# Two graph layers on one core: layer 0's later blocks projected in pairs by seven half products

## The chip, the cores and the metric

The kernel runs on one core of one Trainium2 chip. The metric is the device time of one execution in microseconds (us). A core has a matrix engine (TensorE, PE in the profile), a vector engine (VectorE, DVE), an activation engine (ScalarE, ACT), GpSimd (POOL) and SyncE (SP). In this kernel GpSimd issues the gathers and scatters by index, and SyncE issues the plain transfers. Each engine works through its own queue in order.

## The reference

`x` is 2708 x 1024, `adj` is a 2708 x 2708 matrix of zeros and ones in which most entries are zero; all numbers are float32. Cut to what matters:

```
q, k, v = x @ Wq.T + bq, x @ Wk.T + bk, x @ Wv.T + bv
z    = scale * (q @ k.T) * adj              # zeros count as -10000
x1   = layernorm(x + relu(softmax(z) @ v))  # layer 0
out  = layernorm(x1 + adj @ (x1 @ w1) + b1) # layer 1
```

A row without neighbours gets the mean of all rows of v in layer 0.

## The kernel before, in words

The kernel first turns `adj` into lists of neighbours, in the order of the rows' degrees, and then works on 22 row blocks of 128 rows (the last holds 20). `SLOTS` gives the number of neighbours that a block's rows have at most: 15, 11, 8, 6, 5, 4, 3, 2 for blocks 0 to 7, 13 for block 8, then 5, 4, 4, 3, 3, 3, 2, 2, 2, 1, 1, 1 and 0 for blocks 9 to 21. Blocks 0 and 8 are the widest; some rows with very many neighbours (the "hub" rows) have their shares spread over extra rows.

Layer 0 is rearranged so that there are two products per block. With M = Wq^T Wk (scaled, tile `m_sb`), `y_block` computes y = x M for a block and writes it to DRAM (`y_d`; `yo` is its tile). With y a block's scores need no k: `attend` (or `attend_one` for blocks with one slot, `attend_shares` for the hub and block 0) gathers the block's y rows (`yg`, `gather_y`) and its neighbours' x rows (`g`, `gather`), takes each score as a row-wise product on VectorE (`score`), does the softmax on VectorE and ScalarE, and sums the neighbours' x rows with those weights into `r` (ScalarE makes the first term, VectorE adds the others). Because the weights of a row add up to one, softmax @ v = r @ Wv.T + bv. So each block needs one product more: `flip` turns r by eight transposes into `rT`, `project` makes 16 matmuls (two banks of 128x512, eight each) with `wv_sb`, and `finish0` adds bv to the two banks, does relu and the residual in one instruction over 128x1024, normalises (`norm`) and scatters the rows to `x1_d`. Block 21 takes the mean (`project_mean`).

The order of layer 0 is written out in `steps`: ("y", b) is a block of y, ("v", b) a projection. The y rows 8 to 21 alternate with the projections of blocks 6, 5, 4, 3, 2 and 1; behind the last y (block 21) come the projections of 0, 7, 20, 19, 18, 21, 17, 16, 15, 14, 8, 13, 9, 12, 10 and 11. A small planner hands out the gather-and-softmax pieces (`jobs`, and `late_jobs`, which need every row of y and so wait until y ends) beside the steps: each step adds `STEP` = 14.7 to a credit, and each piece takes its estimated VectorE time from it (`SLOT`, `SMALL`, `END`). `RB` = 3 buffers hold the r tiles. Instructions under `tc.high_priority(URGENT)` are put early on their engine's queue: the additions that read a bank are among them.

Neighbours are gathered into 9 buffers (`G1`); once y has ended, a second pool of 6 (`g2`) is added, until layer 1. Behind y, w1's eight row strips are loaded into the slot of M, one per step (line 1005), and one subtraction over 128x2048 (t1, line 1011) prepares layer 1 within layer 0.

Layer 1 (`work1`) projects neighbour sums of x1. It takes blocks in pairs (`units`), where a pair is a 2 x 2 arrangement of halves: with A = (a11 a12; a21 a22), one row of it per block and each half 512 deep, and w1 in quarters (w11 t1; w21 w22), seven half products (`half_products`, 4 matmuls of 128x512 each) stand for eight. For this, four sums and differences of the turned blocks (`S`, lines 1109 to 1112), three more differences of w1's quarters (t2, t3, t4, lines 1178 to 1180) and additions out of the banks on VectorE (lines 1135 and 1140) are needed. All matmuls of layer 1 are on line 1117.

Lines that the prediction uses: 318 matmuls of y, 322 their additions, 348 gathers, 696 transposes, 719 matmuls of `project`, 771 scores, 828 accumulation of r, 864 and 866 bias and relu with residual, 754 to 767 `norm` (767 is its last ScalarE step), 840 and 848 first and later terms of sums with equal weights, 1086 copies of the bias into layer 1's residual tiles, 1079 neighbour sums of layer 1.

Of the kernel before, what the change touches and what calls it, by code (L numbers as in the profile page):

```python
# [31 lines left out]
SLOTS = [15, 11, 8, 6, 5, 4, 3, 2] + [13, 5, 4, 4, 3, 3, 3, 2, 2, 2, 1, 1, 1, 0]  # L32
MIXED = [7]
# [46 lines left out]
def sparse_part(ctx, tc, x, xT, adj, wqT, wkT, wvT, bq, bk, bv, w1, b1, out):  # L80
# [30 lines left out]
    with es:  # L111
# [24 lines left out]
        wq_i = wm_pool.tile([P, DC, D], F32, name="wq_i", tag="m")  # L136
        wk_i = wk_pool.tile([P, DC, D], F32, name="wk_i")
        for c in range(DC):
            nc.sync.dma_start(out=wq_i[:, c, :], in_=wqT[c * P:(c + 1) * P, :])
# [63 lines left out]
        loaded, sorted_, products = [], [], []  # L203
# [31 lines left out]
        wq_o = wv_pool.tile([P, DC, D], F32, name="wq_o", tag="v")  # L235
        wk_o = wb.tile([P, DC, D], F32, name="wk_o")

        def flip_w(dst, src):

            n = 0  # L240
            for c in range(DC):
                for g in range(DC // 4):
                    tr = p_tr.tile([P, 4, P], F32, name="tr")
                    for k in range(4):
                        o = g * 4 + k
                        nc.tensor.transpose(tr[:, k, :], src[:, c, o * P:(o + 1) * P], ident)  # L246
                    to = dst[:, g * 4:g * 4 + 4, c * P:(c + 1) * P]
                    if n % 2:
                        nc.vector.tensor_copy(to, tr)
                    else:  # L250
                        nc.scalar.copy(to, tr)
                    n += 1

        flip_w(wq_o, wq_i)
        flip_w(wk_o, wk_i)
        load_adj()
        load_adj()
        for c in range(DC):
            nc.vector.scalar_tensor_tensor(junk[:, :D], wq_i[:, c, :], scale, bk_bc, op0=ALU.mult,
                                           op1=ALU.mult, accum_out=u_col[:, c:c + 1])  # L260
# [27 lines left out]
        def y_block(b):  # L288
# [9 lines left out]
            if b == NB - 1:  # L298
# [3 lines left out]
                with tc.high_priority(URGENT):  # L302
                    for c in range(DC):
                        for g in range(G):
                            nc.tensor.matmul(po[g * HUB:(g + 1) * HUB, :YW // G], xt[:, c, :HUB],
                                             m_sb[:, c, g * YW // G:(g + 1) * YW // G], start=(c == 0), stop=(c == DC - 1))
# [8 lines left out]
            for h, (k0, k1) in enumerate(y_cuts):  # L315
                po = p_o.tile([P, HALF], F32, name="po")
                for c in range(DC):
                    put = nc.tensor.matmul(po[:, :k1 - k0], xt[:, c, :], m_sb[:, c, k0:k1], start=(c == 0), stop=(c == DC - 1))  # L318
                    if c == 0:
                        firsts.append(put)  # L320
# [186 lines left out]

        def sort_begin(f):
# [84 lines left out]
        m_sb = wm_pool.tile([P, DC, YW], F32, name="m_sb", tag="m")  # L593
        nc.vector.memset(m_sb[:, :, D:], 0.0)
        nc.vector.tensor_copy(m_sb[:, :, D], u_col)
        done = 0
        for i in range(DC):
            for h in range(NH):
                hs = slice(h * HALF, (h + 1) * HALF)
                po = p_o.tile([P, HALF], F32, name="po")  # L600
                for o in range(DC):
                    nc.tensor.matmul(po, wq_o[:, o, i * P:(i + 1) * P], wk_o[:, o, hs],  # L602
                                     start=(o == 0), stop=(o == DC - 1))
                nc.scalar.copy(m_sb[:, i, hs], po)
# [17 lines left out]
        for b in range(FAMILY):  # L622
# [6 lines left out]
            if b == FAMILY - DC // 2 - 3:  # L629
                wv_sb = wv_pool.tile([P, DC, D], F32, name="wv_sb", tag="v")  # L630
            elif FAMILY - DC // 2 - 2 <= b < FAMILY - 2:
                for c in range(2 * (b - FAMILY + DC // 2 + 2), 2 * (b - FAMILY + DC // 2 + 2) + 2):
                    put = nc.sync.dma_start(out=wv_sb[:, c, :], in_=wvT[c * P:(c + 1) * P, :])
                    follow(put, products[-2])
# [14 lines left out]
        gps = [es.enter_context(tc.tile_pool(name="g0", bufs=G1, reuse_waits="tile"))]  # L649
        turns = [0]  # L650
# [5 lines left out]
        def g_tile():  # L656

            turns[0] += 1
            pool = gps[turns[0] % len(gps)]
            return pool.tile([P, D], F32, name="g", tag="g")  # L660

        def g_clear(pool, n):

            for _ in range(n):
                nc.gpsimd.memset(pool.tile([P, D], F32, name="g", tag="g"), 0.0)

        with tc.high_priority(URGENT):
            g_clear(gps[0], G1)
# [45 lines left out]
        def project(rT, w):  # L714
            po = []
            for h in range(NH):
                acc = p_o.tile([P, HALF], F32, name="po")
                for c in range(DC):
                    put = nc.tensor.matmul(acc, rT[:, c, :], w[:, c, h * HALF:(h + 1) * HALF],  # L719
# [5 lines left out]
        def project_mean(rT, w):  # L725

            acc = p_o.tile([P, HALF], F32, name="po")
            with tc.high_priority(URGENT):
                for c in range(DC):
                    for g in range(G):  # L730
                        nc.tensor.matmul(acc[g * HUB:(g + 1) * HUB, :D // G], rT[:, c, :],
                                         w[:, c, g * D // G:(g + 1) * D // G], start=(c == 0), stop=(c == DC - 1))
# [13 lines left out]
        def norm(t, sm, n, sm2=None):  # L746
# [20 lines left out]
            nc.scalar.activation(t[:n], t[:n], AF.Identity, bias=nmr[:n], scale=rstd[:n])  # L767
# [17 lines left out]
        def attend(b, got):  # L785
# [4 lines left out]
            for i, (j0, j1) in enumerate(cut):  # L790
# [33 lines left out]
                else:  # L824
                    r = wp.tile([P, D], F32, name="r", bufs=RB)
# [45 lines left out]
        def attend_shares(b, got):  # L871
# [9 lines left out]
            for i, (j0, j1) in enumerate(pieces(J)):  # L881
# [25 lines left out]
                if i < len(pieces(J)) - 1:  # L907
# [24 lines left out]

        nc.sync.dma_start(out=bias_bc, in_=bv.to_broadcast([P, D]))
        STEP, Y_END, END, SLOT, SMALL = 14.7, 2.8, 3.3, 2.6, 1.5
        got, xb_bc = {}, []
        w1_left = list(range(DC))
# [3 lines left out]
        late_jobs = [7] + single[::-1] + [17, 16, single[2], 15, single[1], 14, single[0], 8, 8, 8, 13, 9, 12, 10, 11]  # L940
# [3 lines left out]
                 ("y", 15), ("v", 2), ("y", 16), ("y", 17), ("v", 1), ("y", 18), ("y", 19), ("y", 20), ("y", 21)]  # L944
        steps += [("v", b) for b in [0, 7] + single[::-1] + last + [17, 16, 15, 14, 8, 13, 9, 12, 10, 11]]
        assert sorted(b for k, b in steps if k == "v") == list(range(NB))
# [18 lines left out]
        credit = 0.0  # L965
        turned = {}
        pending = None
        left_y = NB - FAMILY
        for i, (kind, b) in enumerate(steps):
            if pending is not None:  # L970
                finish0(*pending)
                pending = None
                credit -= END
            credit += STEP
# [7 lines left out]
            ahead = [c for k, c in steps[i:i + 2] if k == "v" and c not in turned]  # L982
            for c in [c for k, c in steps[i:i + 3] if k == "v" and c not in turned and not (left_y and c in late)]:
                while c not in got and c != 0:
                    credit -= run_job()
            while jobs and credit > 0 and len([c for c in got if c not in turned and c not in last and c != "hub"]) < RB - 1:
# [3 lines left out]
            for c in ahead:  # L990
                turned[c] = turn0(c)
            if kind == "y":
# [3 lines left out]
                if left_y == 0:  # L996
                    xa.release()
                    xb_pool = tc.alloc_tile_pool(name="xb", bufs=1, side="right", reuse_waits="tile")
                    xb_bc.append(xb_pool.tile([P, D], F32, name="xb_bc"))
                    bcast_rows(xb_bc[0], xbT)  # L1000
                    gps.append(tc.alloc_tile_pool(name="g2", bufs=6, side="right", reuse_waits="tile"))
                    w1_sb = wm_pool.tile([P, DC, D], F32, name="w1_sb", tag="m")
            if not left_y and i >= 24 and len(w1_left) > 0:
                c = w1_left.pop(0)
                put = nc.sync.dma_start(out=w1_sb[:, c, :], in_=w1[c * P:(c + 1) * P, :])
                follow(put, products[-1])
            if i == len(steps) - 2:

                w11, t1 = w1_sb[:, :DC // 2, :HALF], w1_sb[:, :DC // 2, HALF:]
                w21, w22 = w1_sb[:, DC // 2:, :HALF], w1_sb[:, DC // 2:, HALF:]  # L1010
                nc.vector.tensor_sub(t1, t1, w11)
            if kind == "v":
                xr = gather_x(x, b)
                pending = b, (project_mean if b in last else project)(turned[b], wv_sb), xr
        finish0(*pending)
        assert not jobs and not w1_left
# [35 lines left out]
        gps.pop().release()  # L1052
        xb_pool.release()
        wv_pool.release()
        cp = tc.alloc_tile_pool(name="c", bufs=1, side="right", reuse_waits="tile")
        cq = tc.alloc_tile_pool(name="cq", bufs=1, side="right", reuse_waits="tile")
        t2, t3, t4 = [cq.tile([P, DC // 2, HALF], F32, name=f"t{k}") for k in (2, 3, 4)]
# [4 lines left out]
        assert sorted(last + [b for unit in units for b in unit]) == list(range(NB))  # L1062
        firsts = []
# [18 lines left out]
        def gather_x1(b, k=0):  # L1082
# [3 lines left out]
            nc.scalar.copy(xr[:n], bias1[:n])  # L1086
# [12 lines left out]
        def turn1(unit, rs):  # L1099

            A = []
            for b, r in zip(unit, rs):
                rT = (cp if A else wp).tile([P, DC, P], F32, name="rT", bufs=2)
                A.append(flip_shares([(part, to_h), (r, to_0)], rT) if b == 0 else flip(r, rT))
            if len(unit) == 1:
                return A, None
            (a11, a12), (a21, a22) = [(a[:, :DC // 2], a[:, DC // 2:]) for a in A]
            S = [cp.tile([P, DC // 2, P], F32, name=f"s{i}") for i in range(4)]
            nc.vector.tensor_add(S[0], a21, a22)
            nc.vector.tensor_sub(S[1], S[0], a11)  # L1110
            nc.vector.tensor_sub(S[2], a11, a21)
            nc.vector.tensor_sub(S[3], a12, S[1])
            return A, S

        def half_products(acc, a, w, start=True, stop=True):
            for k in range(DC // 2):
                nc.tensor.matmul(acc, a[:, k], w[:, k], start=start and k == 0, stop=stop and k == DC // 2 - 1,  # L1117
                                 skip_group_check=True)

        def halves_of(t):  # L1120
            return t[:, :HALF], t[:, HALF:]

        def work1(unit, A, S, xrs):


            ts = [wp.tile([P, D], F32, name="t", tag="t" if k % 2 == 0 else "yg") for k, _ in enumerate(unit)]
            sums = [[stat.tile([P, 1], F32, name=f"sm{h}", bufs=6) for h in range(NH)] for _ in unit]
            a11, a12 = A[0][:, :DC // 2], A[0][:, DC // 2:]

            def bank():  # L1130
                return p_o.tile([P, HALF], F32, name="po")

            def add(to, acc, what):
                with tc.high_priority(URGENT):
                    nc.vector.tensor_add(to, acc, what)  # L1135

            def whole(k, h, acc, what):

# [4 lines left out]
            x0 = halves_of(xrs[0])  # L1143
# [372 lines left out]
```

## Time and profile before

| | us |
|---|---|
| median of 3 runs | 1109.32 |
| lowest and highest run | 1108.97, 1109.59 |
| the profiled execution | 1109.92 |
| span of the profiled execution | 1108.0 |
| TensorE busy | 1033.3 (93%) |
| VectorE busy | 785.7 (71%) |
| GpSimd busy | 473.0 (43%) |
| ScalarE busy | 427.1 (39%) |

The granted clock of TensorE was 0.981 of full speed over the span. Stages, by the span's own clock: lists, M and weights until about 195 us; y of blocks 0 to 7 until about 270; y of blocks 8 to 21 with projections until 555.9; the projections behind y until 786.5; a gap on TensorE until 800.3 with the last normalisation, its scatter and layer 1's first gathers; layer 1's products until about 1090; the last normalisation until 1108.0.

A profile row gives the engine, the line, the operation, output and inputs by the program's names with the shape, the number of instructions or records, and in brackets the idle time ahead of it with what released it. Float32 matmuls leave two records each, so 16 matmuls are "x32".

### The profile page before, as it was taken

To read this page: it belongs to the slowest core of one execution; us is meant where nothing else is said; L and a number is where in the kernel's file an instruction comes from. 1 tells how busy PE (TensorE), PEld (TensorE's weight loads), DVE (VectorE), ACT (ScalarE), POOL (GpSimd) and SP (SyncE) were. 2 spreads that over 40 slices of the span, in tenths; PEclk is the share of its full clock that TensorE was granted. 3 is DMA by queue.
4 is the path that set the end of the run, shared out by engine and by line. 5 is a ranking of instruction groups with operands and counts; after the bars stand their busy time and mean duration, and the time that the engine had idled before them with its cause. 6 is when DMAs were issued, how large, how long until landed. Compare 5 with 4: busy or idle time off the path is not lost.

```text
span 1108.0 us, 10733 instructions
## 1 busy us (share of the span) xinstructions
PE 1033.3 (93%) x3233; PEld 549.3 (50%) x3233; DVE 785.7 (71%) x1712; ACT 427.1 (39%) x896; POOL 473.0 (43%) x397
## 2 busy tenths in 40 slices
PE   7999999999788899999999999999588999999993
PEld 6444466656454455465654444444244444445441
DVE  8799999960677879982166699952268877996531
ACT  4688687312121223232343243332422353323322
POOL 1000320077453456541056377320286778787400
PEclk9999999999999999999999999999798999999997
DMA  9555478426685656644158469521298769989611
GB/s 363 197 203 201 157 241 273 154 77 179 245 275 168 219 187 223 216 142 156 32 186 282 141 211 327 176 97 55 83 282 268 224 188 321 282 271 309 177 46 41
DMA packets 83107, 218.22 MB, mean 197 GB/s; under 512 B 15290, under 2 KB 37274, under 8 KB 80332
## 3 DMA queue, kind: packets, MB, share of 16 engines
q0 software_dynamic: 48768, 148.05, 41.6%
q1 hardware_dynamic: 34272, 69.40, 18.8%
q8 instruction: 27, 0.44, 0.2%
q14 instruction: 40, 0.33, 0.1%
HBM read 208.60 MB, written 33.68 MB: 219 GB/s over the span
## 4 chain that ended last, share of the span: by engine, by line
PE 34%; DVE 25%; issue 18%; DMA 11%; POOL 7%; ACT 2%; POOLq 0%; SPq 0%; DVEq 0%
PE po L719 17%; PE po L318 6%; PE po L1117 6%; DVE a L221 6%; DVE few L224 6%; DMA g<-x_d,tabs 4%; DMA g<-in_x_dram,tabs 3%; POOL g L348 2%; DVE junkv L771 2%; DVE r L1079 2%; PE tr L696 1%; POOL tab_d L558 1%; POOL xr L342 1%; DVE r L828 1%; PE tr L246 1%
## 5 line engine op out<-in xcount | busy, mean ns | idle before, releaser
L318 PE MATMUL po<-m_sb,xt 128*128 128x343 f32 (+1 forms) x1008 | 298.3, 456 | 13.1 <-DVE yo L322 8.3
L719 PE MATMUL po<-wv_sb,rT 128*128 128x512 f32 x672 | 292.3, 593 | 7.0 <-DVE yo L322 3.3
L318 PEld LDWEIGHTS po<-m_sb,xt 128*128 128x128 f32 x1008 | 191.2, 191 | 114.3 <-DVE yo L322 10.9
L719 PEld LDWEIGHTS po<-wv_sb,rT 128*128 128x128 f32 x672 | 126.3, 190 | 161.0 <-issue 154.8
L771 DVE SCALAR_TENSOR_TENSOR junkv<-yg,g 128x1024 uint8<-128x1024 f32 x109 | 132.9, 1219 | 46.4 <-DMA yg<-y_d,tabs 20.0
L348 POOL DMA_INDIRECT g<-in_x_dram,tabs x86 | 106.3, 1236 | 91.1 <-DVE yo L309 28.5
L1079 DVE SCALAR_TENSOR_TENSOR r<-g,valid,r 128x1024 f32<-128x1024 f32 x77 | 98.6, 1281 | 20.2 <-DMA g<-x_d,tabs 19.8
L602 PE MATMUL po<-wk_o,wq_o 128*128 128x512 f32 x256 | 110.5, 592 | 0.0
L754 ACT ACTIVATE junks<-t,lnm 128x1024 uint8<-128x1024 f32 (+1 forms) x43 | 49.4, 1149 | 117.3 <-DVE lnm L750 63.5
L331 ACT ACTIVATE junka<-xt 128x128 f32<-128x128 f32 x176 | 53.9, 306 | 101.4 <-PE po L318 50.9
L1117 PE MATMUL po<-w_sb,rT 128*128 128x512 f32 x192 | 87.2, 598 | 0.0
L348 POOL DMA_INDIRECT g<-x_d,tabs x67 | 76.1, 1136 | 22.7 <-issue 14.0
L828 DVE SCALAR_TENSOR_TENSOR r<-g,pr,r 128x1024 f32<-128x1024 f32 x64 | 81.8, 1279 | 1.6 <-ACT r L826 1.2
L767 ACT ACTIVATE t<-t,nmr,rstd 128x1024 f32<-128x1024 f32 (+1 forms) x43 | 52.9, 1239 | 72.9 <-DVE nmr L766 68.2
L558 POOL DMA_INDIRECT tab_d<-rec,pos_i x22 | 25.1, 1140 | 129.7 <-DVE pos_i L547 123.3
L224 DVE MAX8 few<-a 128x8 f32<-128x75 f32 (+3 forms) x132 | 78.9, 616 | 0.0
L1117 PE MATMUL po<-t,s 128*128 128x512 f32 x160 | 74.5, 610 | 4.0 <-DVE xr L1135 4.0
L602 PEld LDWEIGHTS po<-wk_o,wq_o 128*128 128x128 f32 x256 | 48.4, 190 | 59.3 <-issue 59.0
L1117 PE MATMUL po<-w_sb,s 128*128 128x512 f32 x160 | 72.1, 592 | 0.0
L221 DVE SCALAR_TENSOR_TENSOR a<-a,iota 128x2708 f32<-128x2708 f32 (+1 forms) x22 | 65.2, 2962 | 5.4 <-ACT junk L220 5.4
L864 DVE TENSOR_TENSOR t<-po,bias_bc 128x512 f32<-128x512 f32 (+1 forms) x44 | 30.1, 686 | 50.8 <-PE po L719 50.4
L219 ACT ACTIVATE junk<-a 128x2708 uint8<-128x2708 f32 (+1 forms) x22 | 54.1, 2458 | 28.9 <-DMA a<-in_adj_dram 24.3
(320 smaller groups left out, 1243.1 us busy)
## 6 DMA issues: line engine op xcount, KB each, us to landing
a<-in_adj_dram SPq DMA_DIRECT2D x21, 1354.0 KB, 6.0
y_d<-yo SPq DMA_DIRECT2D x21, 514.0 KB, 6.4
xt<-in_xT_dram SPq DMA_DIRECT2D x21, 512.0 KB, 4.6
wq_i<-in_wqT_dram SPq DMA_DIRECT2D x8, 512.0 KB, 4.5
wk_i<-in_wkT_dram SPq DMA_DIRECT2D x8, 512.0 KB, 11.1
wv_sb<-in_wvT_dram SPq DMA_DIRECT2D x8, 512.0 KB, 6.6
w_sb<-in_w_dram SPq DMA_DIRECT2D x8, 512.0 KB, 3.3
g<-in_x_dram,tabs POOLq DMA_INDIRECT x86, 5.6
```

Source lines behind the costliest of these rows:

```text
L219: nc.scalar.activation(junk[:n], a[:n], AF.Sign, accum_out=cnt[:n, b:b + 1])
L221: nc.vector.scalar_tensor_tensor(a[:n], a[:n], 1.0, iota[:n], op0=ALU.is_equal, op1=ALU.mult)
L224: nc.vector.max(few[:n, i * 8:(i + 1) * 8], a[:n, cuts[i]:cuts[i + 1]])
L318: put = nc.tensor.matmul(po[:, :k1 - k0], xt[:, c, :], m_sb[:, c, k0:k1], start=(c == 0), stop=(c == DC - 1))
L331: put = nc.scalar.activation(junka, xts[b][:, c, :], AF.Copy, accum_out=xs[:, c, b:b + 1])
L348: nc.gpsimd.indirect_dma_start(out=dst[:n], out_offset=None, in_=src, in_offset=bass.IndirectOffsetOnAxis(ap=at, axis=0), bounds_check=N - ...
L602: nc.tensor.matmul(po, wq_o[:, o, i * P:(i + 1) * P], wk_o[:, o, hs], start=(o == 0), stop=(o == DC - 1))
L719: put = nc.tensor.matmul(acc, rT[:, c, :], w[:, c, h * HALF:(h + 1) * HALF], start=(c == 0), stop=(c == DC - 1))
L771: nc.vector.scalar_tensor_tensor(junkv[:n], yg[:n, :D], scale, xg[:n], op0=ALU.mult, op1=ALU.mult, accum_out=s)
L828: nc.vector.scalar_tensor_tensor(r[:n], xg[j][:n], pr[:n, j:j + 1], r[:n], op0=ALU.mult, op1=ALU.add)
L1079: nc.vector.scalar_tensor_tensor(r[:n], xg[:n], ok[:n, j:j + 1], r[:n], op0=ALU.mult, op1=ALU.add)
L1117: nc.tensor.matmul(acc, a[:, k], w[:, k], start=start and k == 0, stop=stop and k == DC // 2 - 1, skip_group_check=True)
```

## The change

Behind the last y the fourteen blocks 7 to 20 go in seven pairs: (7, 20), (19, 18), (17, 8), (16, 11), (15, 10), (9, 14), (13, 12). A pair is computed as in layer 1, by seven half products with the quarters of Wv (11, 12 less 11, 21, 22) and three more differences of them, so four subtractions over 128x2048 are made once, at the first pair. Each pair makes four sums of its turned halves (in one buffer, `s_all`). Its relu, residual and row sum run by halves (`finish_pair`). `pair_products` and `turn_pair` serve both layers; the last pair of either layer runs its products in another order, with a bank of its own for the last one (`first_alone`).

Block 1's projection moves from between y 17 and y 18 to behind y, ahead of block 0's. The planner's credit starts at -`STEP`, a pair adds 2 x `STEP` - `P_END`, the order of `late_jobs` is a new one, and up to three waiting r tiles are allowed behind y (two before). The second neighbour pool (`g2`) is gone: 9 buffers hold the gathers throughout. Block 8's r, and the pair's second rT and t, lie in the pool `xb` that opens when y ends.

Wq, M and Wv are held in four quarter tiles each; Wv arrives in 16 transfers instead of 8. w1 is not loaded into M's slot during layer 0 but into the quarters of Wv once they have been read for the last time, in four transfers; its t1 is subtracted at the start of layer 1, ahead of t2, t3 and t4, which lie where Wv's differences were. Layer 1's bias copies come behind the last normalisation of layer 0 on ScalarE.

The diff, cut to its core:

```diff
+ALONE = [8]
...
-        wv_sb = wv_pool.tile([P, DC, D], F32, name="wv_sb", tag="v")
+        wv_q = quarters_of("wv")
...
-                    r = wp.tile([P, D], F32, name="r", bufs=RB)
+                    r = xb_pools[0].tile([P, D], F32, name="r") if b in ALONE else wp.tile([P, D], F32, name="r", bufs=RB)
...
+        def turn_pair(flips, pool):
+            A = []
+            for k, flip_to in enumerate(flips):
+                rT = (pool if k else wp).tile([P, DC, P], F32, name="rT", bufs=2)
+                A.append(flip_to(rT))
...
+            s_all = wm_pool.tile([P, 4, DC // 2, P], F32, name="s_all", tag="m3")
+            S = [s_all[:, i] for i in range(4)]
+            nc.vector.tensor_add(S[0], a21, a22)
+            nc.vector.tensor_sub(S[1], S[0], a11)
+            nc.vector.tensor_sub(S[2], a11, a21)
+            nc.vector.tensor_sub(S[3], a12, S[1])
+            return A, S
...
+        def pair_products(A, S, w, ts, base, to, whole, first_alone=False):
+            (w11, t1), (w21, w22) = w
+            t2, t3, t4 = ts
+            (a11, a12), a22 = halves_of_turned(A[0]), halves_of_turned(A[1])[1]
+            pa, pb, pc = bank(), bank(), bank()
+            half_products(pa, a11, w11, stop=False)
+            add(to[0][0], pa, base[0][0])
+            half_products(pb, a12, w21)
+            whole(0, 0, pb, to[0][0])
...
+            half_products(pa, S[1], t2, start=False, stop=False)
+            add(to[0][1], pa, base[0][1])
+            half_products(pc, S[0], t1, stop=False)
+            add(to[1][1], pc, base[1][1])
+            half_products(pa, S[2], t3, start=False, stop=False)
+            whole(1, 1, pa, to[1][1])
+            half_products(pc, S[3], w22, start=False)
+            whole(0, 1, pc, to[0][1])
+            products.append(half_products(pa, a22, t4, start=False))
+            whole(1, 0, pa, base[1][0])
...
+        def finish_pair(pair, ts):
+            for k, (b, t) in enumerate(zip(pair, ts)):
+                xr, sums = pair_x[b], [stat.tile([P, 1], F32, name=f"sm{h}", bufs=6) for h in range(NH)]
+                for h in (0, 1) if k == 0 else (1, 0):
+                    th = halves_of(t)[h]
+                    nc.vector.scalar_tensor_tensor(th, th, 0.0, halves_of(xr)[h], op0=ALU.max, op1=ALU.add, accum_out=sums[h])
+                norm(t, sums[0], P, sums[1])
+                scatter(x1_d[:, :], b, P, t, "x1")
...
-        late_jobs = [7] + single[::-1] + [17, 16, single[2], 15, single[1], 14, single[0], 8, 8, 8, 13, 9, 12, 10, 11]
+        pairs = [(7, 20), (19, 18), (17, 8), (16, 11), (15, 10), (9, 14), (13, 12)]
+        late_jobs = [7, 20, 8, 19, 18, 8, 17, 8, 16, 11, 15, 10, 20, 9, 14, 19, 13, 12, 18]
...
-                 ("y", 15), ("v", 2), ("y", 16), ("y", 17), ("v", 1), ("y", 18), ("y", 19), ("y", 20), ("y", 21)]
-        steps += [("v", b) for b in [0, 7] + single[::-1] + last + [17, 16, 15, 14, 8, 13, 9, 12, 10, 11]]
+                 ("y", 15), ("v", 2), ("y", 16), ("y", 17), ("y", 18), ("y", 19), ("y", 20), ("y", 21)]
+        steps += [("v", b) for b in [1, 0] + last] + [("p", pair) for pair in pairs]
...
-        credit = 0.0
+        credit = -STEP
...
+            if kind == "p" and b == pairs[0]:
+                (q11, q12), (q21, q22) = wv_q
+                wv_t = differences()
+                nc.vector.tensor_sub(q12, q12, q11)
+                nc.vector.tensor_sub(wv_t[0], q22, q12)
+                nc.vector.tensor_sub(wv_t[1], wv_t[0], q11)
+                nc.vector.tensor_sub(wv_t[2], q21, wv_t[0])
...
-                    gps.append(tc.alloc_tile_pool(name="g2", bufs=6, side="right", reuse_waits="tile"))
-                    w1_sb = wm_pool.tile([P, DC, D], F32, name="w1_sb", tag="m")
...
-                nc.vector.tensor_sub(t1, t1, w11)
...
+        w1_q = quarters_of("w1")
+        for i in range(2):
+            for j in range(2):
+                nc.sync.dma_start(out=w1_q[i][j], in_=w1[i * HALF:(i + 1) * HALF, j * HALF:(j + 1) * HALF].rearrange(
+                    "(c p) n -> p c n", p=P))
...
-            nc.scalar.copy(xr[:n], bias1[:n])
+            follow(nc.scalar.copy(xr[:n], bias1[:n]), last_norm, same=True)
...
-        follow(nc.vector.tensor_sub(t2, w22, t1), firsts[0], same=True)
+        follow(nc.vector.tensor_sub(t1, t1, w11), firsts[0], same=True)
+        nc.vector.tensor_sub(t2, w22, t1)
```

## The prediction

> **What bounds the kernel now.** I read the page's busy rows and slices first, then the chain of waits, then windows of the stage that changes, then single instructions around it.
>
> ```profile
> PE 1033.3 (93%) x3233; PEld 549.3 (50%) x3233; DVE 785.7 (71%) x1712; ACT 427.1 (39%) x896; POOL 473.0 (43%) x397
> ...
> PE   7999999999788899999999999999588999999993
> ...
> DVE  8799999960677879982166699952268877996531
> ```
>
> TensorE (PE) is at 9 tenths in nearly every slice of 27.7 us, so the page says "PE bound". VectorE's (DVE) row matters as much here: it has slack at 500–550 (digits 2, 1), 6 to 7 behind that, and then three slices of 9 (637–720 us): inside the stage that the change rebuilds, a second engine is already full for a while.
>
> The chain of waits from 640 to 732 us is TensorE alone, block after block:
>
> ```profile
> 642.30 13.74 PE po L719 x32
> 656.03 0.87 PE tr L696 x8
> 656.91 13.74 PE po L719 x32
> ```
>
> One block is a turning of r (8 transposes, 0.87 us) and 32 records (16 matmuls of 128x512) in 13.74 us: 14.61 us. A half product (4 matmuls, 8 records) is a quarter of that, 3.43 us; in layer 1 the same eight records follow each other at 838.74, 842.18 and 845.61, the same 3.43. The windows give the stage behind y and its two parts:
>
> ```profile
> 500.00:550.00 50.00, 50.00 (x199) 30.55 (x201) 8.78 (x28) 13.47 (x59) 3.90 (x4) 1.00 0.29 95
> 555.90:786.50 230.60, 228.53 (x705) 109.78 (x705) 154.53 (x334) 80.14 (x150) 99.12 (x80) 1.00 0.54 179
> 563.30:641.00 77.70, 75.63 (x266) 35.65 (x264) 53.81 (x123) 25.98 (x52) 38.07 (x34) 1.00 0.62 204
> 641.00:730.40 89.40, 89.40 (x252) 42.76 (x251) 86.19 (x174) 33.63 (x66) 51.12 (x37) 1.00 0.69 228
> ```
>
> Columns: window, length, busy time (and instructions) of PE, PEld, DVE, ACT, POOL, then the granted clock, DMA share, GB/s. TensorE idles 2.1 of 230.6 us. VectorE is busy 86.19 of 89.40 in the second part, but 53.81 of 77.70 in the first: there it waits. The last sum of rows (r) of layer 0 ends at 730.34 and is turned only at 758.13, so VectorE is 28 us ahead when the stage closes. That slack is what the change spends.
>
> **TensorE's side.** Seven pairs each lose one half product: 7 x 3.43 = 24.0 us. Block 1's 14.61 us move from between y rows to behind y: y ends at 555.94 - 14.6 = 541.3 instead, and the stage behind it gets 14.6 longer. If VectorE never delayed it, TensorE would end layer 0's products at 541.3 + 230.6 + 14.6 - 24.0 - 2.1 = 760.4, against 786.5: 26 us earlier. Pair 1 would begin at about 581.4.
>
> **VectorE's side.** I added up the instructions that stand between the first accumulation of block 7's r (first behind y) and the last r, at the spacings of this trace: score or accumulation 1.19 to 1.20, 128x512 addition 0.61, 128x2048 2.19, a half with its reader 0.65, small ones 0.13. Before: 141 us. In the changed kernel's own order: 174 us. The 33 more are: the four differences of Wv's quarters at 2.19 (8.8) less w1's t1 = 2.2, which goes to layer 1; block 1's two additions, its relu and its norm, about 3.2, now behind y; and per pair four S additions (2.4), seven additions from banks in place of four, and four halves in place of two whole rows, some 4.5 more than two single blocks, for about five pairs ahead of the last r (22.5).
>
> In the dense part the rows of before that sum to 83.8 us took 86.1 (644.25 to 730.4), a factor of 1.027. The start: y ends at 541.3, the last rows of y land 4 us later, and its gather costs 1.24 of GpSimd and 5.6 to land (both from the page's groups and DMA rows), so the first score is at about 552.1. In before it came 8.6 us behind y's end (564.50), which would make 549.9, the kind bound. From there 170 us of work remain to the last r: 552.1 + 170 x 1.027 = 726.7.
>
> Gathers: the second gather pool is gone, so 9 buffers stand for 15. For each gather I took the VectorE work between the last use of the buffer that it takes over and its own first use; it needs 1.24 + 5.6 = 6.8. Most have 14 to 29. Three early ones (block 17's two, and the first of block 8's last piece) have 6.2, 5.0 and 3.1; one gather of y near the end has 5.3. They stall in turn, not in sum: 3.7 + 1.5 = 5.2 us. So the last r, block 12's, is there at about 732.
>
> **Where they meet.** The transposes of pair 7's two blocks stand within pair 6, the second one behind at least its first half product. Behind that transpose are at most six half products of pair 6 and all seven of pair 7: 0.9 + 13 x 3.43 = 45.5 us. Unstalled, TensorE would want the last r at about 715; it gets it 17 us later. So the 26 us shrink: 732 + 0.3 + 45.5 = 778, against 786.5, **8.5 us earlier**. TensorE then idles some 17 us in the pair stage where it idled 2; the first such wait is in pair 1, whose second bank addition stands behind the differences (about 600 us), some 5 us.
>
> The other edits. Behind the last product, the relu and residual run on halves (0.65 for 1.22), and the bias copy of layer 1 no longer goes ahead of the last normalisation:
>
> ```profile
> 791.14 1.04 ACT L1086 COPY xr<-bias 128x1024 f32<-128x1024 f32 x1 [0.48 <-DMA bias<-in_b_dram]
> 792.10 1.24 ACT L767 ACTIVATE t<-t,nmr,rstd 128x1024 f32<-128x1024 f32 x1
> ```
>
> nmr was ready at 791.49, so the copy cost 0.6; together -1.2 us. w1 arrives in four DMAs behind the last reader of each quarter of Wv, on SP's queue, which has nothing else due there. The last quarter comes free some 3 us before TensorE ends; at 3.3 us per 512 KB (landing, as before) a MB takes 3.3 to 6.6, and 13.5 us pass between TensorE's end (786.5) and layer 1's first transpose (800.26). Hidden; without that cover 4 to 7 us. The subtraction for t1 (2.27) in layer 1's start lies beside gathers; uncovered it costs its 2.27. Wq and m_sb in quarters are names only: 0. Wv's 16 DMAs for 8 are issued while y runs, long before block 6 needs them: 0, and 16 x 0.33 of SP if not. In the pairs, additions wait for banks, and behind a waiting addition stand accumulations; GpSimd's scatters of x1 wait for norms, and behind them stand gathers. Bound: from nothing to twice the gathers' 5 us. Layer 1 else keeps its order; its 4.0 us wait at the second unit stays. I take 0, with 2 us either way.
>
> A row speaks against this change: TensorE restarts slowly after a wait.
>
> ```profile
> 832.75 6.15 PE L1117 MATMUL po<-t,s 128*128 128x512 f32 x8 [4.04 <-DVE xr L1135]
> 838.74 3.60 PE L1117 MATMUL po<-w_sb,rT 128*128 128x512 f32 x8
> ```
>
> Eight records took 6.15 where the next eight took 3.60: 2.55 lost after 4.04 idle, and the clock row of the page falls to 7 there. The rebuilt stage will have such waits. Since VectorE and not TensorE is late, a slow restart is absorbed, except in the last two pairs, where one would cost 2.5: the sum goes by 0, the range by 2.5. [...]
>
> Sum, against the profiled execution (1109.92 us; span 1108.0): -8.5 - 1.2 = -9.7, so 1100.2. The median of the runs, 1109.32, is 0.6 lower: about 1100.
>
> **Rivals.**
> TensorE stays the bound. VectorE catches up, and the whole 26 us + 1.2 is kept: 1082. For it: VectorE has 28 us in hand at the stage's end, and 41 idle us at 500–550. Against: late jobs need every y row landed, so that idle time can't be used, and the 28 us are overdrawn: 33 more work, in a need that comes earlier. Chance 0.08.
>
> Slower: gathers and waits in one chain. The price is that every us of lateness of the last r goes one to one to the end, and the point of decision is the last r at 786.5 + 1.2 - 45.8 = 742, 10 us later than my forecast. For it: the first part behind y, where VectorE idled 24 of 77.7 us although it had 15 buffers (longest waits 3.5 for y's gather, 6.8 for ACT's r); the same 24 again, in place of my 5.2, puts the last r at 751 and the time at 1109.3 + 9 = 1118; 40 us would make 1134. Against: 6.6 of those 24 were waits for TensorE's banks, which a late VectorE does not have. Chance 0.22.
>
> No change: some 15 us of such waits; 1107 to 1111. Chance 0.12.
>
> **Numbers.** My forecast, 0.58, has its own range: a start 2 us earlier, no stall (-5), layer 1 ±2 on one side; twice the stall, one slow restart and layer 1's 2 on the other: 1092 to 1107. For 8 in 10 it reaches into the slower case and a little towards the full gain: 1089 to 1115. 0.2% (2.2 us) is about what a measurement of this kernel can tell from no change. Faster by more: 0.58 + 0.08 = 0.66; same 0.12; slower 0.22.
>
> **What would show it.** In the profile after: y's last product at 541 (else the move isn't what I think); seven stretches of 56 records in pairs, 3.43 per half product; VectorE 9 in the slices from 555 to 735; TensorE waits of some 17 us in all, released by VectorE's rows (r, or the bank additions), the first near 600; the last r at 732 and the last product's end at 778. Waits on VectorE "<-DMA g" or "yg" of over 15 us in sum would say that the slower rival is right; a TensorE without waits, ending near 760, the first one. A wait of layer 1's first products for w1 would make a term of mine wrong that I put at 0.

## The result and the profile after

The changed kernel takes 1092.1 us (median of four runs, 1090.77 to 1093.59); the kernel before, run beside it, 1109.45. The ratio is 0.984, 95% interval 0.982 to 0.986: faster by 1.6%, where 1100 had been forecast. The profiled execution took 1092.7 us, its span 1091.0.

The page of after, busy rows and slices (a slice is now 27.3 us):

```profile
PE 1015.2 (93%) x3177; PEld 540.1 (50%) x3177; DVE 826.3 (76%) x1801; ACT 428.1 (39%) x896; POOL 486.7 (45%) x397
...
PE   7999999999798989999998999999589999999993
...
DVE  8799999980487789965297999984477777896431
```

TensorE's busy time fell by 18.1 us, VectorE's rose by 40.6. VectorE's row now has a 9 in the slice at 546 us and 9s in the four slices from 600 to 709, with a 7 between them; before, its three 9s stood from 637 to 720. The windows of after, the two of before again and the stretch between the first pair's wait and the last r:

```profile
563.30:641.00 77.70, 71.19 (x255) 33.93 (x254) 69.40 (x134) 26.72 (x51) 47.12 (x30) 0.96 0.47 149
641.00:730.40 89.40, 88.29 (x253) 42.07 (x252) 88.37 (x209) 39.05 (x75) 51.69 (x41) 1.00 0.69 230
600.00:724.50 124.50, 122.30 (x332) 57.53 (x332) 122.12 (x269) 47.66 (x89) 72.92 (x56) 0.98 0.67 223
```

The busy time of VectorE is the third after the window's length, behind two of TensorE: 69.40 of 77.70 where before had 53.81, and from 600 to 724.5 both engines are busy 98% of the time. The timeline of TensorE in after shows one long wait in the whole pair stage, and its slow restart:

```profile
592.87 1.88 PE L958 MATMUL po<-wv,rT 128*128 128x512 f32 x4
601.26 6.07 PE L958 MATMUL po<-t,s_all 128*128 128x512 f32 x8 [6.51 <-DVE t L970]
...
608.89 3.60 PE L958 MATMUL po<-t,s_all 128*128 128x512 f32 x8
...
724.86 1.06 PE L698 MATMUL tr<-ident,r 128*128 128x128 f32 x8 [0.17 <-DVE r L831]
...
766.96 3.60 PE L958 MATMUL po<-t,rT 128*128 128x512 f32 x8
770.40 0.28 PE L1160 MATMUL tr<-some,ones 128*128 128x1 f32 x2
783.14 1.94 PE L698 MATMUL tr<-ident,r 128*128 128x128 f32 x8 [12.47 <-DVE r L1189]
```

The row at 770.40 is a small matmul straight behind layer 0's last product, and the one at 783.14 is layer 1's first transpose. The same two in before:

```profile
786.48 0.28 PE L1047 MATMUL tr<-some,ones 128*128 128x1 f32 x2
800.26 1.94 PE L696 MATMUL tr<-ident,r 128*128 128x128 f32 x8 [13.50 <-DVE r L1077]
```

So layer 0's products end 16.1 us earlier. The row at 724.86 turns block 12's r, the last one; VectorE's accumulation for it is

```profile
723.44 1.28 DVE L831 SCALAR_TENSOR_TENSOR r<-g,pr,r 128x1024 f32<-128x1024 f32 x1
```

with the next instruction at 724.63, the time that I take for its end. The gap to layer 1 is 12.7 us (13.8 before), and from there to the end of the span it is 307.9 (307.7). So 16.1 + 1.0 - 0.1 = 17.0, the difference of the spans.

Behind the long wait stands a chain over three engines. VectorE:

```profile
587.91 2.27 DVE L1091 TENSOR_TENSOR t<-t,wv 128x2048 f32<-128x2048 f32 x1
...
590.17 2.27 DVE L1092 TENSOR_TENSOR t<-wv,t 128x2048 f32<-128x2048 f32 x1
...
592.44 1.26 DVE L831 SCALAR_TENSOR_TENSOR r<-g,pr,r 128x1024 f32<-128x1024 f32 x1
600.51 1.29 DVE L970 TENSOR_TENSOR t<-po,bias_bc 128x512 f32<-128x512 f32 x2 [6.81 <-DMA x_d<-t,tabs]
```

The first bank addition of pair 1 writes a t tile. Its buffer was block 0's t, whose rows must have been scattered first: VectorE waits 6.81 us for that DMA. GpSimd's queue, in which the scatter stands:

```profile
582.51 4.29 POOL L343 DMA_INDIRECT xr<-in_x_dram,tabs  x1 [3.52 <-DVE t L869]
587.11 7.48 POOL L349 DMA_INDIRECT g<-in_x_dram,tabs  x1 [0.30 <-DVE rstd L767]
594.89 0.93 POOL L343 DMA_INDIRECT xr<-in_x_dram,tabs  x1 [0.30 <-issue]
596.13 1.00 POOL L685 DMA_INDIRECT x_d<-t,tabs  x1 [0.30 <-issue]
```

Block 0's rows were normalised at 589.25 (ScalarE's step at 588.01 takes 1.24), but the scatter went out at 596.13, because one gather ahead of it took 7.48 us. The median gather behind y takes 1.08. The first row shows that a residual load was slow too, 4.29 us, and no 128x2048 instruction ran beside that one. VectorE worked there without a gap on an accumulation, the first pair's four sums and small instructions:

```profile
582.84 1.26 DVE L851 SCALAR_TENSOR_TENSOR r<-g,valid,r 128x1024 f32<-128x1024 f32 x1
584.03 0.67 DVE L947 TENSOR_TENSOR s_all<-rT 128x512 f32<-128x512 f32 x1
...
586.03 0.67 DVE L950 TENSOR_TENSOR s_all<-rT,s_all 128x512 f32<-128x512 f32 x1
```

### The profile page after: what moved, and what is told of

It is laid out like the page before. It is cut to its first block, busy times and chain, and to the rows that moved or that the text cites. A ratio compares the mean times of both kernels' runs of the same rounds, so it can differ in the third digit from the quotient of the medians.

```text
span 1091.0 us, 10751 instructions
## 1 busy us (share of the span) xinstructions
PE 1015.2 (93%) x3177; PEld 540.1 (50%) x3177; DVE 826.3 (76%) x1801; ACT 428.1 (39%) x896; POOL 486.7 (45%) x397
## 3 DMA queue, kind: packets, MB, share of 16 engines
q1 hardware_dynamic: 36384, 69.40, 18.8%
## 4 chain that ended last, share of the span: by engine, by line
DVE 32%; PE 28%; issue 18%; DMA 10%; POOL 7%; ACT 3%; POOLq 0%; DVEq 0%; ACTq 0%
PE po L958 17%; PE po L319 6%; DVE few L225 6%; DVE a L222 5%; DVE junkv L774 5%; DMA g<-in_x_dram,tabs 4%; DVE r L831 3%; PE po L721 2%; POOL g L349 2%; DVE t L970 1%; POOL tab_d L563 1%; DMA g<-x_d,tabs 1%; DMA yg<-y_d,tabs 1%; PE tr L247 1%; POOL xr L343 1%
## 5 line engine op out<-in xcount | busy, mean ns | idle before, releaser
L349 POOL DMA_INDIRECT g<-in_x_dram,tabs x86 | 114.3, 1330 | 76.4 <-ACT r L829 25.2
L958 PE MATMUL po<-t,s_all 128*128 128x512 f32 x272 | 126.6, 609 | 10.6 <-DVE t L970 6.5
L721 PE MATMUL po<-wv,rT 128*128 128x512 f32 x224 | 101.7, 611 | 6.2 <-DVE yo L323 2.8
L958 PEld LDWEIGHTS po<-t,s_all 128*128 128x128 f32 x272 | 52.6, 196 | 78.2 <-issue 61.1
L958 PE MATMUL po<-w,rT 128*128 128x512 f32 x192 | 87.9, 607 | 0.0
L721 PEld LDWEIGHTS po<-wv,rT 128*128 128x128 f32 x224 | 43.2, 195 | 60.0 <-issue 53.5
L958 PE MATMUL po<-w,s_all 128*128 128x512 f32 x160 | 72.1, 592 | 0.0
```

The lines of the kernel that those rows point to most:

```text
L349: nc.gpsimd.indirect_dma_start(out=dst[:n], out_offset=None, in_=src, in_offset=bass.IndirectOffsetOnAxis(ap=at, axis=0), bounds_check=N - ...
L721: put = nc.tensor.matmul(acc, rT[:, c, :], w[c // 4][h][:, c % 4, :], start=(c == 0), stop=(c == DC - 1))
L958: put = nc.tensor.matmul(acc, a[:, k], w[:, k], start=start and k == 0, stop=stop and k == DC // 2 - 1, skip_group_check=True)
```

## The experiments

To compare stages I use, beside the time, the stretch from y's last addition to layer 0's last product in each profile: 230.5 us in before, 230.2 in after, where block 1's 14.6 us are in it as well. The last additions of y, in before and in after:

```profile
555.94 0.52 DVE L322 TENSOR_TENSOR yo<-po,y_bc 128x343 f32<-128x343 f32 x1 [1.17 <-PE po L318]
```

```profile
540.25 0.52 DVE L323 TENSOR_TENSOR yo<-po,y_bc 128x343 f32<-128x343 f32 x1 [1.17 <-PE po L319]
```

The end of y itself spreads by some us between profiles of the same instructions (555.9 in before, 551.1 in the last experiment, which is the same up to there), so this stretch is the steadier measure.

**The t tiles of odd and even pairs in different pools.** The edit, on the changed kernel:

```diff
-            ts = [(xb_pools[0] if k else wp).tile([P, D], F32, name="t", bufs=2) for k in range(2)]
+            t_pool = wp if pairs.index(pair) % 2 else xb_pools[0]
+            ts = [t_pool.tile([P, D], F32, name="t", bufs=2) for k in range(2)]
```

> In the profile after, TensorE's one long wait in the pair stage (6.51 us at 594.7, then eight records in 6.07 instead of 3.60) hangs on VectorE's first bank addition of pair 1, which waited 6.81 us for the scatter of block 0, because pair 1's t takes that block's buffer. Here the t tiles of odd and even pairs lie in different pools, so that pair 1 takes buffers that nobody uses. Theory (this one wait is what is left of the gain): layer 0's products end 7 to 9 us earlier, at 761 to 763, time 1083 to 1086. Rival 1 (VectorE's amount of work decides, and the wait only fell into slack): TensorE waits later in the stage instead, under 3 us gained, 1089 to 1092. Rival 2 (GpSimd's queue is late as a whole, so the next gather takes the wait over): 1092, with waits for g or yg of some 5 us.

1084.81 us, ratio to before 0.978 (0.973 to 0.982); the stretch is 223.0. The last product ended at 761.58. TensorE has no wait over 1.3 us left in the stage, and the largest is again for an r:

```profile
716.04 1.06 PE L698 MATMUL tr<-ident,r 128*128 128x128 f32 x8 [1.26 <-DVE r L831]
```

The wait for the scatter was worth 7.1 us of the stretch. The first bank addition also stood ahead of the last two subtractions here (584.94 against 586.82 and 589.68), so the run removes the wait and what stood in front of the addition together. Rivals 1 and 2 fall: the gain is over 3 us, and no wait for gathers took its place (0.9 us in sum). The wait stood in VectorE's own row of work, and the last r ended at 715.8, so this run does not tell TensorE's wait from VectorE's row; the doubled sums below do. GpSimd was held up here too, and block 0's scatter went out at 593.08, but nothing waited for that tile:

```profile
587.09 5.68 POOL L343 DMA_INDIRECT xr<-in_x_dram,tabs  x1 [0.67 <-DVE nmr L769]
```

**The subtractions in another form.**

```diff
-                nc.vector.tensor_sub(q12, q12, q11)
-                nc.vector.tensor_sub(wv_t[0], q22, q12)
-                nc.vector.tensor_sub(wv_t[1], wv_t[0], q11)
-                nc.vector.tensor_sub(wv_t[2], q21, wv_t[0])
+                for to, a_, b_ in ((q12, q12, q11), (wv_t[0], q22, q12), (wv_t[1], wv_t[0], q11), (wv_t[2], q21, wv_t[0])):
+                    nc.vector.scalar_tensor_tensor(to, a_, 1.0, b_, op0=ALU.mult, op1=ALU.subtract)
```

> The scatter of block 0 was ready at 589.3 but issued at 596.1: GpSimd's gather ahead of it took 7.48 us where the median gather takes 1.08, and it ran beside the four 128x2048 subtractions of VectorE. Here these four are written as scalar_tensor_tensor with the same result. Theory A (the plain two-tile TENSOR_TENSOR holds GpSimd up): that gather takes 1 to 2.5 us, the scatter goes out 5 us earlier, TensorE's wait of 6.5 shrinks to about 1, time 1084 to 1088. Theory B (any dense VectorE work holds it up, or something else does): the gather stays at 5 us or more, time 1091 to 1094.

1093.32 us, 0.984 (0.980 to 0.989), stretch 230.6: nothing changed, and the gather took 7.48 us again:

```profile
586.57 7.48 POOL L349 DMA_INDIRECT g<-in_x_dram,tabs  x1 [0.30 <-DVE rstd L767]
```

So it does not matter which of the two forms the instruction has.

**Two of the subtractions left out.** On the changed kernel:

```diff
-                nc.vector.tensor_sub(wv_t[1], wv_t[0], q11)
-                nc.vector.tensor_sub(wv_t[2], q21, wv_t[0])
+                wv_t = [wv_t[0]] * 3
```

> The changed kernel without the third and fourth subtraction over 128x2048 (t2 is read in the place of t3 and t4 in layer 0, so layer 0's numbers differ). Theory A (these wide subtractions hold up GpSimd's gather beside them, 7.48 us): that gather takes 1 to 2.5 us, block 0's scatter is issued near 590, TensorE's long wait shrinks from 6.5 to under 2, time 1083 to 1087. Theory B (the gather is slow for another reason): it takes 5 us or more again, and VectorE waits even longer for the scatter, 9 to 11 us.

This kernel leaves out two of the differences, so its layer 0 isn't the layer asked for; it serves the timing alone. One run: 1084.86 us, stretch 224.8. That VectorE has 4.4 us less work is in this time too. The gather at the same place, and the first bank addition:

```profile
585.86 2.94 POOL L349 DMA_INDIRECT g<-in_x_dram,tabs  x1 [0.30 <-DVE rstd L767]
589.11 0.95 POOL L343 DMA_INDIRECT xr<-in_x_dram,tabs  x1 [0.30 <-issue]
590.37 1.00 POOL L685 DMA_INDIRECT x_d<-t,tabs  x1 [0.30 <-issue]
```

```profile
594.73 1.29 DVE L970 TENSOR_TENSOR t<-po,bias_bc 128x512 f32<-128x512 f32 x2 [1.75 <-DMA x_d<-t,tabs]
```

7.48 - 2.94 = 4.5 us, the 4.4 of the two subtractions. They held GpSimd up, in whichever form. (2.94 is a little over the 2.5 that theory A named, and well over the median of 1.08: VectorE was busy without a gap beside this gather too, with a relu over 20x1024 and accumulations over 128x1024.)

The gather of after ended 0.9 us behind VectorE's last instruction in the row (594.59 against 593.70). By what means the subtractions hold GpSimd up, no run shows.

**Block 1's move alone**, on the kernel before:

```diff
-                 ("y", 15), ("v", 2), ("y", 16), ("y", 17), ("v", 1), ("y", 18), ("y", 19), ("y", 20), ("y", 21)]
-        steps += [("v", b) for b in [0, 7] + single[::-1] + last + [17, 16, 15, 14, 8, 13, 9, 12, 10, 11]]
+                 ("y", 15), ("v", 2), ("y", 16), ("y", 17), ("y", 18), ("y", 19), ("y", 20), ("y", 21)]
+        steps += [("v", b) for b in [1, 0, 7] + single[::-1] + last + [17, 16, 15, 14, 8, 13, 9, 12, 10, 11]]
```

> The kernel before, with block 1's projection moved behind y and nothing else. Theory (TensorE's work is only moved, and VectorE has 28 us in hand there): 1107 to 1111, no change. Rival (the move itself is a part of the gain, since the late gathers start 15 us earlier and nothing then waits for y): 1102 to 1106.

1107.44 us, 0.9987 (0.996 to 1.0013): no difference that can be told, as the theory had it. The stretch is 243.2 = 230.5 + 14.6 - 1.9; the 2.1 us that TensorE idled behind y in before are gone, since the extra block covers them.

**Block 1 put back**, in the changed kernel:

```diff
-                 ("y", 15), ("v", 2), ("y", 16), ("y", 17), ("y", 18), ("y", 19), ("y", 20), ("y", 21)]
-        steps += [("v", b) for b in [1, 0] + last] + [("p", pair) for pair in pairs]
+                 ("y", 15), ("v", 2), ("y", 16), ("y", 17), ("v", 1), ("y", 18), ("y", 19), ("y", 20), ("y", 21)]
+        steps += [("v", b) for b in [0] + last] + [("p", pair) for pair in pairs]
```

> The changed kernel, with block 1's projection put back between y 17 and y 18 and nothing else. y ends 14.6 us later, and with it every late score. Theory (VectorE's row of work from y's end to the last r decides in the pair kernel; its last r was only just in time at 724.6): the last r comes 14.6 later less block 1's additions and norm (3) and less the scatter wait (up to 6.8), so 5 to 12 us later than after: 1097 to 1104, with TensorE waits of 8 us or more released by VectorE. Rival (TensorE alone bounds the stage, the move is indifferent): 1091 to 1094.

1096.36 us, 0.988 (0.983 to 0.992). That is just under the theory's 1097 and above the rival's 1094; the interval overlaps that of after, but the four runs (1093.72 to 1098.48) all lie above after's four (1090.77 to 1093.59). The trace agrees: the stretch is 221.3, and without block 1 after's would be 230.2 - 14.6 = 215.6, so 5.7 are lost. TensorE waited 10.5 us in all, where it had waited 7.6. The first of the three longest waits is again the one for the first pair's t; the other two are new:

```profile
599.90 6.27 PE L958 MATMUL po<-t,s_all 128*128 128x512 f32 x8 [5.10 <-DVE t L970]
623.50 1.98 PE L958 MATMUL po<-wv,s_all 128*128 128x512 f32 x4 [2.73 <-DVE s_all L947]
...
731.45 1.94 PE L698 MATMUL tr<-ident,r 128*128 128x128 f32 x8 [1.49 <-DVE r L831]
```

The rest of the 5.7 are records that took longer. The move that is worth nothing by itself is worth some 5 us to the pairs: it gives VectorE its late work earlier (here y ended 13.7 us later than in after, and the last r some 14).

**Eight half products in each pair**, without the four sums and the differences, all else kept:

```diff
-            if len(flips) == 1:
+            if len(flips) == 1 or pool is xb_pools[0]:
                 return A, None
...
-            pair_products(A, S, wv_q, wv_t, [bias, bias], [halves_of(t) for t in ts], whole, pair == pairs[-1])
+            for k, a in enumerate(A):
+                for h in range(NH):
+                    acc = bank()
+                    half_products(acc, a[:, :DC // 2], wv_q[0][h], stop=False)
+                    put = half_products(acc, a[:, DC // 2:], wv_q[1][h], start=False)
+                    whole(k, h, acc, bias[h])
+            products.append(put)
...
-                nc.vector.tensor_sub(q12, q12, q11)
-                nc.vector.tensor_sub(wv_t[0], q22, q12)
-                nc.vector.tensor_sub(wv_t[1], wv_t[0], q11)
-                nc.vector.tensor_sub(wv_t[2], q21, wv_t[0])
```

> The changed kernel with everything kept but the seven products: each pair makes eight half products with Wv itself, without the four sums of turned halves and without the differences of Wv. Theory (the gain is the 24.0 us of half products less TensorE's 10 idle or slow us): TensorE ends layer 0 at 770.4 + 24.0 - 10 = 784, time 1104 to 1108, VectorE with slack again. Rival (the gain comes from the new order, block 1's place and the finish by halves): 1092 to 1100.

1121.69 us, 1.011 (1.008 to 1.013): slower than the kernel before (1111.29 beside it), and nearly 16 more than the middle of the theory's 1104 to 1108. The stretch is 258.4, 28.3 above after's. Instead of after's wait there are three others that I had not foreseen, 9.8 us in all, with slow restarts:

```profile
612.76 0.66 PE L698 MATMUL tr<-ident,r 128*128 128x128 f32 x4 [3.24 <-ACT rT L699]
613.25 29.33 PE L958 MATMUL po<-wv,rT 128*128 128x512 f32 x64
...
648.77 1.11 PE L698 MATMUL tr<-ident,r 128*128 128x128 f32 x4 [4.88 <-ACT rT L699]
649.68 29.93 PE L958 MATMUL po<-wv,rT 128*128 128x512 f32 x64
...
683.05 27.63 PE L958 MATMUL po<-wv,rT 128*128 128x512 f32 x64
```

The 64 records behind the two longer waits took 29.33 and 29.93 us, the next 64 took 27.63; with a slow transpose some 4.5 us were lost. Without its waits and slow restarts the stretch is 244.1, which is 24.0 above after's 220.1 counted in the same way: the seven half products.

Here both blocks' transposes stand in a row between pairs, and their copies to SBUF wait in ScalarE's queue behind a first term of r that waits for VectorE (ScalarE idles 4.53 us until 609.72, and copies from 612.14 on). So the rest of the change gains nothing in this form: without the seven products it is 10.4 us slower than the kernel before, and its waits and slow restarts are 14.3. What the rest would be worth in an order without such waits stays open.

**The sums of the turned halves twice**, on the variant with two pools:

```diff
-            nc.vector.tensor_add(S[0], a21, a22)
...
+            for _ in range(2 if pool is xb_pools[0] else 1):
+                nc.vector.tensor_add(S[0], a21, a22)
...
```

> The variant with the t tiles in two pools (1084.8), with the four sums of each layer-0 pair computed twice: 2.4 us more VectorE work per pair, 14.6 ahead of the last r, nothing more for TensorE. Theory (VectorE's row of work up to the last r sets the end, as the forecast had it): the last r comes 12 to 15 later and the end with it, 1096 to 1100. Rival (TensorE bounds the stage and VectorE was only just in time by its place in the queue): 1085 to 1089.

1094.35 us, 0.986 (0.983 to 0.990), 9.5 more than the variant and a little under the theory's 1096; stretch 232.2 (+9.2). The last r ended at 730.2 instead of 715.8: 14.4 later, 12.6 without the 1.8 by which y ended later. The end followed by 3.4 us less, since here the last transpose stands one half product further on (42.1 us ahead of the end, not 45.5). The added work is VectorE's alone, and the end moves: VectorE decides. TensorE waited 0.65 us for a sum itself and 7.6 ahead of transposes of an r, so it is the rows up to the r that were late.

**Fewer gather buffers in the variant, and one more** (`G1 = 7`, `G1 = 10`):

> The variant with the t tiles in two pools (1084.8), with 7 gather buffers in place of 9. The forecast had 9 buffers at their edge (5.2 us of stalls), the profile after showed none. If 9 are near the edge: waits of VectorE for g of 8 us or more behind y, and more in layer 1, time 1092 to 1105. If they are far from it: 1084 to 1087.

> The variant with the t tiles in two pools (1084.8), with 10 gather buffers in place of 9. Seven buffers cost 11.7 us, of which 7.0 were lost while y was computed (y's end at 545.5 instead of 538.5) and 5 behind it. If the ninth buffer is still short for the y stage: y ends 1 to 3 us earlier, 1081 to 1084. If 9 are enough: 1084 to 1086.

Seven: 1096.51 us, 0.987 (0.985 to 0.988), stretch 228.0 (+5.0), and y ends 7.0 later. The time is as expected for buffers near their edge, but VectorE waited only 4.9 us in sum for g and yg behind y, not 8. Ten: 1082.31, 0.974 (0.970 to 0.978), the fastest version, but its stretch is the same 223.2; what it gained in its profile lies at y's end (534.3 against 538.5), about the spread of that point between profiles, and the intervals of the two versions overlap. Whether the tenth buffer helps stays open.

**The kernel before without its second gather pool** (the lines with `g2` and its release taken out):

> The kernel before without its second gather pool: 9 buffers behind y in place of 15, nothing else. Theory (the second pool only let VectorE run ahead into 28 us of slack, so that taking it away is free): 1108 to 1112. Rival (the late gathers fall behind, TensorE waits for r): 1115 to 1125, with TensorE idle behind y over 5 us.

1107.08 us, 0.998 (0.996 to 1.001), stretch 230.0 against 230.5: free, as expected. VectorE's waits for g and yg behind y rose from 14.8 us to 26.2, and its slack took them up: TensorE waited once for an r, 1.50 us.

## Why the prediction was right, and where its sizes were off

**TensorE's sum.** 230.5 + 14.6 - 24.0 - 2.1 = 219.0 for the stretch without waits; after's 230.2 less its waits (6.5, 0.7, 0.2, 0.2) and the slow restart (2.5) is 220.1. Right to 1 us. With eight half products in each pair, the 24.0 came back.

**The last r, the term that was mis-sized.** Forecast 732, measured 724.6, which is 7.4 of the 7.9 us by which the median was missed. Its parts: the first score came at 551.2 (forecast 552.1). The 170 us of rows took 173.4 to the end of the last r, but 8.7 of that were waits, so the work took 164.7, not 174.6: the factor 1.027 came from a stretch that held 3.2 us of waiting itself, and about half of the small instructions stand 0.07 apart where I had counted 0.13 for all. The waits that I had counted, 5.2 for gathers, were 0.3. I had named the wrong buffer for each gather: the third tight one went out at 566.58, before the accumulation (568.17) that I had taken for its release.

```profile
566.58 1.80 POOL L349 DMA_INDIRECT g<-in_x_dram,tabs  x1 [0.54 <-DVE ve L764]
```

What came instead, 6.81 for a scatter, I had bounded only in general (scatters wait for norms, gathers behind them), without looking at which buffer a t tile takes. So two errors partly cancelled, and that is luck: work and gathers were put 14.8 us too high, the other waits 8.4 too low. With the scatter's wait gone (the two pools) the last r came at 715.8, and the forecast of 1100 would have been off by twice as much (1084.81).

**From the last r to the end.** 45.5 forecast; 724.86 to 770.40 is 45.5. The tail: 1.2 forecast, 1.0 measured. Layer 1: 0 forecast, 0.1 measured; w1's late loads were hidden.

**TensorE's waits.** 17 us forecast, 7.6 measured. The first, near 600, came where I had put it and a little longer (6.5 for 5), but I had it wait for VectorE's differences; the addition did stand behind them, and then waited for the scatter. Place and size came out; the cause did not.

**The slow restart.** After 6.51 us idle, eight records took 6.07 in place of 3.60: 2.47 lost, near the row of before (2.55) and the 2.5 that the prediction set in its range for one such restart. The granted clock was 0.59 over these eight records and 0.58 over those of before; after a wait of 1.96 us (two of the subtractions left out) eight records took 3.70. The prediction misread the page's clock row there: the slice with that restart shows 8, not 7. (VectorE's three slices from 554 us read 6, not 6 to 7, and the page has no words "PE bound"; no term rests on either.) The slow restart was absorbed, as assumed: TensorE still had to wait 0.17 for the last r.

**The rivals.** "TensorE stays the bound" fails on the last r (TensorE waits for it) and on doubled sums. TensorE's wait for the last r is short, 0.17 us, so in after the two engines come out close together: TensorE, late by its first wait, and VectorE with its last r. The slower rival's chain of waits for gathers didn't come: 0.3 us of such waits where before had 12.3 in its first part. That a loaded VectorE arrives after its gathers fits the kernel before with nine buffers (26.2 us of such waits on a VectorE with slack), but the order of the gathers differs too. The forecast's 8.5 us for the end of the products became 16.1 by the terms above; the gathers are 4.9 of them.

## What to carry to other kernels

When TensorE work is traded for VectorE work, write down for the stage when the last input of TensorE's queue can be ready on the other engine, and how much of TensorE's queue stands behind it: the end is the later of the two sums, and here the second half of that (45.5 us) was exact while the first was 7 off. Calibrate an engine's rate on a stretch without waits, and put waits in by name. For every new tile ask who last used its buffer, stores included: one t tile behind a scatter cost 7 us of a 24 us saving, and moving it to another pool got them back.

## What I had not expected of the hardware

A gather that GpSimd issues in 1.08 us (the median behind y) took 7.48 beside two subtractions over 128x2048 on VectorE, and 2.94 without them; with the two it took 7.48 whether they were written as TENSOR_TENSOR or as SCALAR_TENSOR_TENSOR. It is not width alone: a residual load took 4.29 beside an accumulation and four sums of 128x1024 and 128x512, while from 600 to 724.5 us, with VectorE busy 98% of the time, the median gather took 1.06 and the longest 2.14. What separates the two stretches was not tested.
